# Layer 1 of a two-layer model: rows of four states by 32 channels over segments of 784 columns, on one core

## The chip, the core and the metric

The kernel runs on one core of a Trainium2 chip. The metric is the device time of one execution in microseconds (us). The core has five engines that run their own instruction streams and meet at semaphores: TensorE (PE, with its weight loads as PEld), VectorE (DVE), ScalarE (ACT), GpSimd (POOL) and SyncE (SP), which here issues all DMA transfers. The transfers run on 16 DMA engines. SBUF and PSUM are the memories beside the engines, 128 partitions wide; PSUM is what TensorE writes.

## What is computed

The input x has 16 images of 192 channels and 56 x 56 = 3136 positions. Layer 0 adds a gated recurrence over the positions to x. Layer 1 adds a bidirectional selective scan; the change concerns it alone. Its core, for each of the 384 inner channels d and 16 states n:

```
xc  = silu(conv_b + sum_k xp[:, k:k+L] * conv_w[:, k])       # 4 taps along the positions
dbl = xc @ W_xproj.T                                          # 12 columns for dt, 16 for B, 16 for C
dt  = softplus(dbl[..., :12] @ W_dt.T + dt_bias)
h_t = h_(t-1) * exp(dt_t * A) + (dt_t * x_t) * B_t            # per channel and state
y_t = sum_n h_t * C_t        ;  y = y + xc * D
out = ((y_f + y_b) * silu(z)) @ W_out.T + b_out               # y_f forward, y_b backward over the positions
```

Everything is float32.

## The kernel before

Layer 0 (lines 63 to 535) runs first and leaves two tensors in DRAM: `xmid`, the residual stream, and `xhat`, the normalised input of layer 1.

Layer 1 (from line 541) walks over 224 **steps**: 16 images, forward then backward, 7 segments of T = 448 positions. Each step has 24 **units**: 3 blocks m of 128 channels by 8 pairs p of states. The 128 partitions of a tile are 128 channels, and a unit holds two states side by side, 2 x 448 = 896 columns. For a unit:

- `decay` (L833): ScalarE writes exp(dt * A) for each of the two states into a PSUM tile dA (2 buffers), two instructions.
- `times_b` (L840): GpSimd multiplies the rows of B, broadcast over partitions, with dt*x (tile dtx): dB, 4 buffers.
- `scan` (L845): VectorE runs the recurrence h = dA*h + dB, one instruction a state. The result goes back into dA, or into SBUF tile h for each third unit (`on_pool`).
- `times_c` (L875): h * C gives hC (4 buffers), on VectorE for two units of three and on GpSimd for the third.
- `add_up` (L881): TensorE adds the two states into y of the block by products with the identity, 448 columns each; the block's first unit also adds D * xc and, backward, the forward result yf.
- `keep` (L863): ScalarE copies the last column as the next segment's start.

The order is written by hand (L898 to L916): at iteration u the program issues keep(u-1), decay(u+1), scan(u), times_c, times_b(u+3), add_up(u-2), and then what is listed in `events` for that slot. `prelude(i)` (L645) fills those events. It works one step ahead: slot s of step i falls in the iterations of step i-1. There the input projection px (L668), the convolution pc as four products with diagonal matrices (L688), the gates (three ScalarE instructions in one slot, L637), the projection pp (L725), the write of B and C to DRAM (`bc`, L737) and dt and dtx (L744 to L756) are made, and B and C are read back broadcast over all 128 partitions, two states at a time, with 10 buffers each (`load_rows`, L758). dt and dtx stay in SBUF. After a block's last unit `y_out` (L770) takes y from PSUM; after a backward step `po_mm` and `po_out` make the output.

All engines take their instructions in order, SP too: a load that waits for a buffer holds back every later transfer of that queue. [...]

Of the kernel before, what the change touches and what calls it, by code (L numbers as in the profile page):

```python
# [19 lines left out]
NPR = NS // 2  # L20
DTR = 12
KC = 4
T = 448
# [7 lines left out]
def _bc(ap, n):  # L31

    p, t = ap.shape
    return ap.unsqueeze(1).to_broadcast([p, n, t])
# [3 lines left out]
def tile_wkv_then_bimamba(ctx: ExitStack, tc: tile.TileContext, a: dict, out: bass.AP):  # L38
# [501 lines left out]

    cw = ctx.enter_context(tc.tile_pool(name="l1const", bufs=1))
    ring = ctx.enter_context(tc.tile_pool(name="l1ring", bufs=2))
    pa = ctx.enter_context(tc.tile_pool(name="l1a", bufs=2, space=PSUM))
    py = ctx.enter_context(tc.tile_pool(name="l1y", bufs=2, space=PSUM))
    pm = ctx.enter_context(tc.tile_pool(name="l1mm", bufs=2, space=PSUM))

    ident = cw.tile([128, 128], F32, tag="ident", name="ident")
    make_identity(nc, ident)

# [11 lines left out]
    with tc.tile_pool(name="l1raw", bufs=1) as raw:  # L561
        for n, g, sh in (("W_in_x", "g1", "b1"), ("W_in_z", "g2", "b2")):
            wt = raw.tile([P0, NB0, DI], F32, tag=n, name=n)
            nc.sync.dma_start(out=wt, in_=blocks(a[n]))
            g_t, sh_t = vec(g, [P0, NB0]), vec(sh, [P0, NB0])
            bt = cw.tile([128, NM], F32, tag="bias_" + n, name="bias_" + n)
            for m in range(NM):
                pb = pm.tile([128, 512], F32, tag="mm", name="pb1")
                for c in range(NB0):
                    nc.tensor.matmul(  # L570
                        pb[:, 0:1],
                        wt[:, c, m * 128 : (m + 1) * 128],
                        sh_t[:, c : c + 1],
                        start=c == 0,
                        stop=c == NB0 - 1,
                    )
                nc.vector.tensor_copy(bt[:, m : m + 1], pb[:, 0:1])
            ws = cw.tile([P0, NB0, DI], F32, tag=n + "_g", name=n + "_g")
            for c in range(NB0):
                nc.vector.tensor_scalar(ws[:, c, :], wt[:, c, :], g_t[:, c : c + 1], None, ALU.mult)  # L580
            Win[n], bin_[n] = ws, bt
# [7 lines left out]
    for d in "fb":  # L589
        w = {}  # L590
        cwt = vec(f"conv_w_{d}", [128, NM, KC])
        w["diag"] = cw.tile([128, NM, KC, 128], F32, tag="diag" + d, name="diag" + d)
        for m in range(NM):
            for j in range(KC):
                nc.vector.tensor_scalar(w["diag"][:, m, j, :], ident, cwt[:, m, j : j + 1], None, ALU.mult)
# [9 lines left out]
        w["dtw"] = cw.tile([DTR + 1, DI], F32, tag="dtw" + d, name="dtw" + d)  # L605
        nc.sync.dma_start(out=w["dtw"][0:DTR, :], in_=a[f"W_dt_{d}"])
        for m in range(NM):
            nc.sync.dma_start(
                out=w["dtw"][DTR : DTR + 1, m * 128 : (m + 1) * 128],
                in_=a[f"dt_bias_{d}"][:, m : m + 1].rearrange("p m -> m p"),  # L610
            )
        al = vec(f"A_log_{d}", [128, NM, NS])
        w["A"] = cw.tile([128, NM, NS], F32, tag="A" + d, name="A" + d)
        nc.scalar.activation(w["A"], al, AF.Exp)
        nc.vector.tensor_scalar(w["A"], w["A"], -1.0, None, ALU.mult)
        br.append(w)
    dtr2 = []
    for i in range(2):
        t = cw.tile([DTR + 1, T], F32, tag=f"dtr{i}", name=f"dtr{i}")
        nc.gpsimd.memset(t, 1.0)  # L620
        dtr2.append(t)

    TH = T + KC - 1
    NU = NM * NPR
# [9 lines left out]
    def mm_tile(name):  # L634
        return pm.tile([128, 512], F32, tag="mm", name=name)

    def silu_gate(name, ps, nbias):  # L637

        g = ring.tile([128, T], F32, tag="gate", name=name)
        nc.scalar.activation(g, ps, AF.Exp, bias=nbias, scale=-1.0)  # L640
        nc.scalar.activation(g, g, AF.Ln, bias=1.0)
        nc.scalar.activation(g, g, AF.Exp, scale=-1.0)
        return g

    def prelude(i):  # L645
# [6 lines left out]

        lo, hi = (t0, min(L, t0 + TH)) if bwd else (max(0, t0 - (KC - 1)), t0 + T)
        n = hi - lo
        off = TH - n if not bwd else 0
        st["own"] = 0 if bwd else n - T
        st["xs"], st["xc"], st["dt"], st["dtx"], st["z"] = {}, {}, {}, {}, {}
        st["Bt"], st["Ct"], st["yf"], st["ys"] = {}, {}, {}, {}
# [5 lines left out]
        def load_xh():  # L664
            st["xh"] = ring.tile([P0, NB0, TH], F32, tag="xh", name="xh")
            nc.sync.dma_start(out=st["xh"][:, :, :n], in_=blocks(xhat_d[b])[:, :, lo:hi])

        def px_mm(m):  # L668
            tmp["px", m] = px = mm_tile("px")
            for c in range(NB0):  # L670
                nc.tensor.matmul(  # L671
                    px[:, :n],
                    Win["W_in_x"][:, c, m * 128 : (m + 1) * 128],
                    st["xh"][:, c, :n],
                    start=c == 0,
                    stop=c == NB0 - 1,
                )

        def px_out(m):
            st["xs"][m] = xs = ring.tile([128, TH], F32, tag="xs", name="xs")  # L680
            if n < TH:
                pad = slice(n, TH) if bwd else slice(0, off)
                nc.gpsimd.memset(xs[:, pad], 0.0)
            nc.scalar.activation(
                xs[:, off : off + n], tmp["px", m][:, :n], AF.Identity, bias=bin_["W_in_x"][:, m : m + 1]
            )

        def pc_mm(m):  # L688
            tmp["pc", m] = pc = mm_tile("pc")
            for j in range(KC):  # L690
                o = KC - 1 - j if bwd else j
                nc.tensor.matmul(  # L692
                    pc[:, :T], w["diag"][:, m, j, :], st["xs"][m][:, o : o + T], start=j == 0, stop=j == KC - 1
                )

        def pc_gate(m):
            tmp["gc", m] = silu_gate("gc", tmp["pc", m][:, :T], w["ncb"][:, m : m + 1])

        def pc_out(m):
            st["xc"][m] = xc = ring.tile([128, T], F32, tag="xc", name="xc", bufs=4)  # L700
            nc.vector.scalar_tensor_tensor(
                xc, tmp["pc", m][:, :T], w["cb"][:, m : m + 1], tmp["gc", m], ALU.add, ALU.mult
            )

        def pz_mm(m):
            tmp["pz", m] = pz = mm_tile("pz")
            for c in range(NB0):
                nc.tensor.matmul(
                    pz[:, :T],
                    Win["W_in_z"][:, c, m * 128 : (m + 1) * 128],  # L710
                    st["xh"][:, c, st["own"] : st["own"] + T],
                    start=c == 0,
                    stop=c == NB0 - 1,
                )

        def pz_gate(m):
            tmp["gz", m] = silu_gate("gz", tmp["pz", m][:, :T], nbz[:, m : m + 1])

        def pz_out(m):
            st["z"][m] = z = ring.tile([128, T], F32, tag="z", name="z")  # L720
            nc.vector.scalar_tensor_tensor(
                z, tmp["pz", m][:, :T], bz[:, m : m + 1], tmp["gz", m], ALU.add, ALU.mult
            )

        def pp_mm():  # L725
            tmp["pp"] = pp = mm_tile("pp")
            for m in range(NM):
                nc.tensor.matmul(
                    pp[: 2 * NS + DTR, :T], w["xp"][:, m, :], st["xc"][m], start=m == 0, stop=m == NM - 1
                )  # L730

        def pp_out():
            bcs = ring.tile([2 * NS, T], F32, tag="bcs", name="bcs", bufs=1)
            nc.scalar.copy(bcs, tmp["pp"][0 : 2 * NS, :T])
            nc.scalar.copy(dtr2[i % 2][0:DTR, :], tmp["pp"][2 * NS : 2 * NS + DTR, :T])
            st["bc"] = dramr.tile([2 * NS, T], F32, tag="bc", name="bc")
            nc.sync.dma_start(out=st["bc"], in_=bcs)  # L737

        def pd_mm(m):
            tmp["pd", m] = pd = mm_tile("pd")  # L740
            nc.tensor.matmul(pd[:, :T], w["dtw"][:, m * 128 : (m + 1) * 128], dtr2[i % 2], start=True, stop=True)


        def pd_log(m):  # L744
            tmp["ab", m] = ab = ring.tile([128, T], F32, tag="ab", name="ab")
            nc.scalar.activation(ab, tmp["pd", m][:, :T], AF.Abs)
# [3 lines left out]
        def pd_out(m):  # L750
            st["dt"][m] = dt = ring.tile([128, T], F32, tag="dt", name="dt", bufs=4)
            nc.vector.scalar_tensor_tensor(dt, tmp["pd", m][:, :T], 0.0, tmp["ab", m], ALU.max, ALU.add)  # L752

        def dtx(m):
            st["dtx"][m] = t = ring.tile([128, T], F32, tag="dtx", name="dtx", bufs=4)
            nc.gpsimd.tensor_tensor(t, st["dt"][m], st["xc"][m], ALU.mult)  # L756

        def load_rows(which, p, first):  # L758
            st[which][p] = t = ring.tile([128, 2, T], F32, tag=which, name=which, bufs=10)
            nc.sync.dma_start(out=t, in_=st["bc"][first + 2 * p : first + 2 * p + 2, :].partition_broadcast(128))  # L760

        def load_yf(m):
            st["yf"][m] = t = ring.tile([128, T], F32, tag="yf", name="yf_t")
# [6 lines left out]
        def y_out(m):  # L770
            st["ys"][m] = ys = ring.tile([128, T], F32, tag="ys", name="ys", bufs=4)
            if bwd:
                nc.vector.tensor_tensor(ys, st["y", m][:, :T], st["z"][m], ALU.mult)
                return
            nc.scalar.copy(ys, st["y", m][:, :T])
# [4 lines left out]
        def po_mm(k):  # L780
            tmp["po", k] = po = mm_tile("po")
            for m in range(NM):
                nc.tensor.matmul(
                    po[:P0, :T], Wout[:, m, k * P0 : (k + 1) * P0], st["ys"][m], start=m == 0, stop=m == NM - 1
                )

        def po_out(k):
            if k == 0:
                st["o"] = ring.tile([P0, NB0, T], F32, tag="o", name="o", bufs=1)
            nc.vector.scalar_tensor_tensor(  # L790
                st["o"][:, k, :], tmp["po", k][:P0, :T], bout[:, k : k + 1], st["xmid"][:, k, :], ALU.add, ALU.add
# [177 lines left out]
```

## Time and profile before

| | |
|---|---|
| median of 3 runs | 22,529.4 us (22,524.35 to 22,530.25) |
| profiled execution, its own time | 22,528.8 us |
| its span, first to last instruction | 22,527.0 us |
| mean granted TensorE clock | 0.892 |
| busy: PE, PEld, DVE, ACT, POOL | 82%, 39%, 87%, 57%, 78% |
| DMA: moved, mean | 2557.58 MB, 114 GB/s |
| loads of B and of C (L760) | 2 x 1792 of 448 KB, 6.8 and 6.6 us to landing |

The span is that of one profiled execution. A group of the profile's part 5 gives line, engine, operation, output and inputs with shapes, count, then busy time in us and the mean of one in ns, then the engine's idle time before such instructions and what ended it. In the list of waits the columns are total us, how often, and the longest. In the table by stage each engine has its busy us and its number of instructions; DMA share is the mean busy share of the 16 DMA engines.

### The profile page before, as it was taken

Reading aid. Unit: us, or ns where it says so; the run is one execution under the profiler, and the core shown is the slowest. Engines: PE = TensorE matmul, PEld = TensorE weight load, DVE = VectorE, ACT = ScalarE, POOL = GpSimd, SP = SyncE. Lnnn points to the kernel's source line nnn. Section 1 sums busy time; section 2 is a strip of 40 time slices with the busy share of each in tenths; the row PEclk is TensorE's granted clock in tenths of the full one; section 3 lists DMA queues with packets and bytes.
Section 4 is the critical chain, followed back from the end, with each engine's and each line's share of the span. In section 5 each row is a group of like instructions: output and inputs, shape, how many; then the busy total and the mean of one; then the engine's idle time right before and its main releaser. Section 6 shows DMA issues by size and latency. Waiting matters only on the chain.

```text
span 22527.0 us, 170276 instructions
## 1 busy us (share of the span) xinstructions
PE 18553.1 (82%) x44630; PEld 8710.7 (39%) x44630; DVE 19655.0 (87%) x19088; ACT 12947.8 (57%) x24169; POOL 17544.7 (78%) x9098
## 2 busy tenths in 40 slices
PE   4666666688888888888888888988888888888888
PEld 2333333334343434343434343434343434343433
DVE  5666666499999999999999999999999999999999
ACT  3444544466665656565656565656565656565655
POOL 3455455388888888888888888888888888888888
PEclk7888887889898989898989898989898989898989
DMA  3444443333333333333323333333332333232332
GB/s 119 142 138 142 139 140 130 103 114 104 115 102 114 105 113 105 112 107 109 110 108 112 107 112 107 112 107 112 107 112 107 112 107 112 107 112 107 112 107 98
DMA packets 982787, 2557.58 MB, mean 114 GB/s; under 512 B 120344, under 2 KB 449328, under 8 KB 981808
## 3 DMA queue, kind: packets, MB, share of 16 engines
q1 hardware_dynamic: 981808, 2546.68, 32.8%
q8 instruction: 351, 5.75, 0.1%
q14 instruction: 628, 5.14, 0.1%
HBM read 2186.57 MB, written 359.66 MB: 113 GB/s over the span
## 4 chain that ended last, share of the span: by engine, by line
PE 39%; DVE 36%; ACT 9%; issue 7%; POOL 5%; DMA 2%; SPq 1%; DVEq 0%; POOLq 0%; ACTq 0%
DVE dA L854 18%; PE y L889 16%; PE pc L692 8%; ACT dA L838 6%; DVE h L854 5%; DVE hC L879 5%; PE px L671 5%; PE pc L109 2%; POOL dB L843 2%; PE pWk L109 2%; POOL hC L879 2%; DVE dt L752 2%; DVE q L336 2%; PE pWv L109 1%; PE y L885 1%
## 5 line engine op out<-in xcount | busy, mean ns | idle before, releaser
L843 POOL TENSOR_TENSOR dB<-Bt,dtx 128x896 f32<-128x896 f32 x5376 | 11169.9, 2083 | 2585.8 <-DVE h L854 1283.9
L889 PE MATMUL y<-hC,ident 128*128 128x448 f32 x21504 | 9762.7, 600 | 2221.4 <-POOL hC L879 2176.8
L854 DVE TENSOR_TENSOR_SCAN dA<-dA,state,dB 128x448 f32<-128x448 f32 x6144 | 7081.2, 1153 | 669.0 <-ACT dA L838 537.2
L889 PEld LDWEIGHTS y<-hC,ident 128*128 128x128 f32 x21504 | 4295.7, 207 | 7168.8 <-issue 3841.5
L879 DVE TENSOR_TENSOR hC<-dA,Ct 128x896 f32<-128x896 f32 x3584 | 3912.6, 1092 | 321.3 <-DVE dA L854 7.2
L838 ACT ACTIVATE dA<-dt,Ab 128x448 f32<-128x448 f32 x5376 | 3422.5, 637 | 1133.3 <-DVE h L854 565.2
L838 ACT ACTIVATE dA<-dt,Af 128x448 f32<-128x448 f32 x5376 | 3421.5, 637 | 805.3 <-DVE hC L879 357.2
L879 POOL TENSOR_TENSOR hC<-h,Ct 128x896 f32<-128x896 f32 x1792 | 3732.9, 2083 | 13.7 <-issue 8.4
L854 DVE TENSOR_TENSOR_SCAN h<-dA,state,dB 128x448 f32<-128x448 f32 x3072 | 3351.0, 1132 | 0.0
L873 ACT COPY state<-dA 128x2 f32<-128x2 f32 x3072 | 485.1, 158 | 4048.5 <-DVE hC L879 4046.5
L336 DVE TENSOR_TENSOR_SCAN q<-a,q,b 128x392 f32<-128x392 f32 x384 | 496.0, 1345 | 903.4 <-ACT b L358 903.4
L671 PE MATMUL px<-xh,W_in_x_g 96*128 96x451 f32 (+1 forms) x2688 | 1239.4, 586 | 26.8 <-DMA xh<-xhat 26.8
L854 DVE TENSOR_TENSOR_SCAN dA<-dA,dB 128x448 f32<-128x448 f32 x1024 | 1119.4, 1093 | 132.5 <-ACT dA L838 105.8
L377 POOL TENSOR_TENSOR gin<-gin,v 128x1176 f32<-128x1176 f32 x128 | 392.0, 3062 | 925.7 <-ACT gin L371 921.7
L692 PE MATMUL pc<-xs,diagf 128*128 128x448 f32 x2688 | 1067.4, 539 | 2.8 <-issue 1.8
L692 PE MATMUL pc<-xs,diagb 128*128 128x448 f32 x2688 | 1065.3, 538 | 0.0
L671 PEld LDWEIGHTS px<-xh,W_in_x_g 96*128 96x128 f32 x2688 | 589.7, 219 | 676.3 <-issue 615.3
L109 PE MATMUL pc<-v,center_w 128*128 128x392 f32 x896 | 433.5, 652 | 446.7 <-DVE v L393 438.5
L756 POOL TENSOR_TENSOR dtx<-dt,xc 128x448 f32<-128x448 f32 x672 | 761.3, 1133 | 19.8 <-DVE dt L752 19.8
L692 PEld LDWEIGHTS pc<-xs,diagf 128*128 128x128 f32 x2688 | 510.3, 190 | 506.6 <-issue 494.0
L692 PEld LDWEIGHTS pc<-xs,diagb 128*128 128x128 f32 x2688 | 508.3, 189 | 504.3 <-issue 479.8
L109 PE MATMUL pc<-xm,center_w 128*128 128x392 f32 x896 | 352.9, 547 | 401.4 <-POOL xm L263 401.1
(156 smaller groups left out, 20434.8 us busy)
## 6 DMA issues: line engine op xcount, KB each, us to landing
Bt<-bc SPq DMA_DIRECT2D x1792, 448.0 KB, 6.8
Ct<-bc SPq DMA_DIRECT2D x1792, 448.0 KB, 6.6
v<-Wv SPq DMA_DIRECT2D x128, 588.0 KB, 5.1
yf<-ys SPq DMA_DIRECT2D x336, 224.0 KB, 1.9
yf_t<-yf SPq DMA_DIRECT2D x336, 224.0 KB, 5.8
xh<-xhat SPq DMA_DIRECT2D x192, 338.2 KB, 6.6
Wk<-k SPq DMA_DIRECT2D x64, 588.0 KB, 3.0
Wv<-ve SPq DMA_DIRECT2D x64, 588.0 KB, 2.9
```

What stands on the lines that cost most here:

```text
L109: nc.tensor.matmul(dst[:, o, :n], wt[:, i, o, :], src[:, i, :n], start=i == ins[0], stop=i == ins[-1])
L336: nc.vector.tensor_tensor_scan(t[:, b, after][:, run], data0(b), data1(b), t[:, b, col : col + 1], op0, op1)
L671: nc.tensor.matmul(px[:, :n], Win["W_in_x"][:, c, m * 128 : (m + 1) * 128], st["xh"][:, c, :n], start=c == 0, stop=c == NB0 - 1,)
L692: nc.tensor.matmul(pc[:, :T], w["diag"][:, m, j, :], st["xs"][m][:, o : o + T], start=j == 0, stop=j == KC - 1)
L752: nc.vector.scalar_tensor_tensor(dt, tmp["pd", m][:, :T], 0.0, tmp["ab", m], ALU.max, ALU.add)
L756: nc.gpsimd.tensor_tensor(t, st["dt"][m], st["xc"][m], ALU.mult)
L838: nc.scalar.activation(dA[u][:, j, :T], st["dt"][m], AF.Exp, scale=br[st["bwd"]]["A"][:, m, n : n + 1])
L843: nc.gpsimd.tensor_tensor(dB[u], st["Bt"][p], _bc(st["dtx"][m], 2), ALU.mult)
L854: nc.vector.tensor_tensor_scan(hs[u][:, j, run], dA[u][:, j, :T][:, run], dB[u][:, j, run], 0.0 if st["first"] else st["before"][:, n : n ...
L873: nc.scalar.copy(nxt["before"][:, n : n + 2].unsqueeze(2), hs[u][:, :, end : end + 1])
L879: eng.tensor_tensor(hC[u], hs[u], st["Ct"][p], ALU.mult)
L889: nc.tensor.matmul(st["y", m][:, :T], ident, hC[u][:, j, :], start=False, stop=p == NPR - 1 and j == 1)
```

## The change

The rows of a tile are no longer 128 channels but four states by 32 channels: partition 32*j + c holds state 4k + j of channel 32q + c of block m. A unit is (m, k, q), k and q from 0 to 3, so 48 units a step, and a segment has T = 784 positions in place of 448, so 4 segments and 128 steps. A unit has one decay, one scan and one product each of 784 columns.

What follows from the layout:

- dt and dtx are needed four times over, once for each state row. They are made as before (128 channels, GpSimd and VectorE), written to DRAM (`dt_d`, `dtx_d`), and read back by `load_rep`, 32 channels repeated fourfold, 4 loads a block each, rings of 6.
- B and C are read back by `load_rows`, four states each repeated for 32 channels, 4 loads each a step, rings of 5.
- The sum over states is a product with `fold`, a 128 x 32 matrix that adds the four state rows of a channel. It writes 32 of the 128 output partitions (column group q of TensorE). Two units are added in one call, with their products alternating between two column groups, in two halves of 392 columns.
- The convolution does the same: xs is written to DRAM with three zero columns at each end, and `load_xs` reads 32 channels shifted by 0 to 3 columns into the four groups of 32 rows (ring of 4); one product with the taps on `fold` replaces four. The input projection is made in forward steps only, since the backward pass reads the same xs.
- One PSUM tile of two banks serves all products of the prelude, and one y. Each gate is split over two slots. times_b runs two units ahead, not three; hC has 5 buffers. B, C and dt columns share one tile.
- The weights are laid out anew at the start of layer 1 with some 130 small loads more.

The diff, cut to its core:

```diff
-T = 448
+T = 784
-def _bc(ap, n):
+def _bc(ap, n, at=1):
     p, t = ap.shape
-    return ap.unsqueeze(1).to_broadcast([p, n, t])
+    return ap.unsqueeze(at).to_broadcast([p, n, t] if at else [n, p, t])
...
-    py = ctx.enter_context(tc.tile_pool(name="l1y", bufs=2, space=PSUM))
-    pm = ctx.enter_context(tc.tile_pool(name="l1mm", bufs=2, space=PSUM))
+    py = ctx.enter_context(tc.tile_pool(name="l1y", bufs=1, space=PSUM))
+    pm = ctx.enter_context(tc.tile_pool(name="l1mm", bufs=1, space=PSUM))
+    HB = T // 2
+    NQ = 4
+    fold = cw.tile([128, 32], F32, tag="fold", name="fold")
...
         def px_out(m):
+            t = row("xin", 1)
...
+            nc.sync.dma_start(out=xs_b[m * 128 : (m + 1) * 128, PAD + t0 : PAD + t0 + T], in_=t)
+        def load_xs(m, q):
+            st["xs"][m, q] = t = row("xs", 4)
+            c0 = m * 128 + q * 32
+            o = t0 + (PAD if bwd else 0)
+            one = xs_b[c0 : c0 + 32, o : o + T]
+            nc.sync.dma_start(out=t, in_=bass.AP(one.tensor, one.offset, [[1, KC], *one.ap]))
         def pc_mm(m):
...
+            for h in range(2):
+                for q in range(NQ):
+                    nc.tensor.matmul(
+                        pc[32 * q : 32 * q + 32, h, :HB],
+                        w["conv"][:, m, q, :],
+                        st["xs"][m, q][:, h * HB : (h + 1) * HB],
...
+                        tile_position=(0, 32 * q),
+                    )
...
         def pd_out(m):
...
+            nc.sync.dma_start(out=st["dt_d"][m * 128 : (m + 1) * 128, :], in_=dt)
         def dtx(m):
...
+            nc.sync.dma_start(out=st["dtx_d"][m * 128 : (m + 1) * 128, :], in_=t)
+        def load_rep(which, m, q):
+            st[which][m, q] = t = row(which, 6)
+            c0 = m * 128 + q * 32
+            nc.sync.dma_start(out=t, in_=_bc(st[which + "_d"][c0 : c0 + 32, :], NQ, 0))
+        def load_rows(which, k, first):
+            st[which][k] = t = row(which, 5)
+            n = first + NQ * k
+            nc.sync.dma_start(out=t, in_=_bc(st["bc"][n : n + NQ, :], 32))
...
+        for m, slot in enumerate((11, 19, 23)):
+            for q in range(NQ):
+                at(slot - (5 if m == 0 else 3), load_xs, m, q)
+            at(slot, pc_mm, m)
...
+        for m, slot in enumerate((29, 37, 41)):
+            at(slot, pd_mm, m)
+            at(slot + 1, pd_abs, m)
+            at(slot + 2, pd_log, m)
+            at(slot + 3, pd_out, m)
+            at(slot + 4, dtx, m)
+        for k in range(NQ):
+            at(32 if k == 0 else 36 + 4 * k, load_rows, "Bt", k, 0)
+            at(33 if k == 0 else 36 + 4 * k, load_rows, "Ct", k, NS)
         for m in range(NM):
+            for q in range(NQ):
+                at(NU + 16 * m + (q - 8 if q < 2 else q - 6), load_rep, "dt", m, q)
+                at(NU + 16 * m + (q - 8 if q < 2 else q - 6), load_rep, "dtx", m, q)
+            at(NU + 16 * m + 19, y_out, m)
+    units = [(st, m, k, q) for st in steps for m in range(NM) for k in range(NQ) for q in range(NQ)]
...
     def decay(u):
+        st, m, k, q = units[u]
+        dA[u] = pa.tile([128, 1024], F32, tag="dA", name="dA")
+        nc.scalar.activation(dA[u][:, :T], st["dt"][m, q], AF.Exp, scale=br[st["bwd"]]["A"][:, m, q, k : k + 1])
     def times_b(u):
+        st, m, k, q = units[u]
+        dB[u] = row("dB", 4)
+        nc.gpsimd.tensor_tensor(dB[u], st["Bt"][k], st["dtx"][m, q], ALU.mult)
...
+    def add_up(us):
+        for h in range(2):
+            cols = slice(h * HB, (h + 1) * HB)
+            for u in us:
+                st, m, k, q = units[u]
+                if k == 0 and q == 0 and h == 0:
+                    st["y", m] = py.tile([128, 2, 512], F32, tag="y", name="y")
+                terms = [(fold, hC[u])]
...
+                for j, (wt, rhs) in enumerate(terms):
+                    nc.tensor.matmul(
+                        st["y", m][32 * q : 32 * q + 32, h, :HB],
+                        wt,
+                        rhs[:, cols],
...
+                        tile_position=(0, 32 * q),
+                    )
...
-            if 0 <= u + 3 < N:
-                times_b(u + 3)
+            if 0 <= u + 2 < N:
+                times_b(u + 2)
...
-            if 0 <= u - 2 < N:
-                add_up(u - 2)
             for fn in events.pop(u, ()):
                 fn()
+            if 0 <= u - 2 < N and u % 2 == 1:
+                add_up((u - 3, u - 2))
```

## Prediction

> **What bounds the kernel now.** I read the totals first, then layer 1 by stage, then who waits for whom, then the costliest groups, and last the DMA queue in a short stretch.
>
> Page, part 1, and busy time by stage (layer 1 begins near 4400 us):
>
> ```profile
> PE 18553.1 (82%) x44630; PEld 8710.7 (39%) x44630; DVE 19655.0 (87%) x19088; ACT 12947.8 (57%) x24169; POOL 17544.7 (78%) x9098
> 4400.00:13000.00 8600.00, 7480.91 (x17464) 3386.08 (x17465) 7987.68 (x7854) 5159.19 (x10372) 7349.34 (x3769) 0.91 0.31 109
> 13000.00:22480.00 9480.00, 8294.31 (x19424) 3756.53 (x19423) 8848.84 (x8703) 5702.70 (x11461) 8108.91 (x4155) 0.92 0.31 109
> ```
>
> Columns of the last two: stretch, length, PE, PEld, DVE, ACT, POOL busy, clock, DMA share, GB/s. Layer 1 takes 22,527 - 4400 = 18,127 us. VectorE is busy 93% of it, GpSimd 86%, the DMA engines 31%. Layer 0 (4400 us) is not touched.
>
> VectorE's waits from 13000 to 22480 us:
>
> ```profile
> DVE dA L854 <- ACT dA L838: 341.9, 371, 1.2
> DVE xc L701 <- ACT gc L642: 44.1, 75, 1.2
> ...
> DVE dA L854 <- POOL dB L843: 3.5, 3, 1.2
> ```
>
> It waits for a decay now and then, for GpSimd hardly ever, and for no transfer. VectorE bounds layer 1.
>
> Groups:
>
> ```profile
> L843 POOL TENSOR_TENSOR dB<-Bt,dtx 128x896 f32<-128x896 f32 x5376 | 11169.9, 2083 | 2585.8 <-DVE h L854 1283.9
> L889 PE MATMUL y<-hC,ident 128*128 128x448 f32 x21504 | 9762.7, 600 | 2221.4 <-POOL hC L879 2176.8
> L854 DVE TENSOR_TENSOR_SCAN dA<-dA,state,dB 128x448 f32<-128x448 f32 x6144 | 7081.2, 1153 | 669.0 <-ACT dA L838 537.2
> L879 DVE TENSOR_TENSOR hC<-dA,Ct 128x896 f32<-128x896 f32 x3584 | 3912.6, 1092 | 321.3 <-DVE dA L854 7.2
> L854 DVE TENSOR_TENSOR_SCAN h<-dA,state,dB 128x448 f32<-128x448 f32 x3072 | 3351.0, 1132 | 0.0
> ```
>
> DMA queue over the whole span, then in 40 slices of 5 us from 13000 to 13200 us:
>
> ```profile
> q1 hardware_dynamic: 981808, 2546.68, 32.8%
> DMA  0000000599885400000000036998680000000000
> GB/s 0 2 3 0 0 0 14 170 288 407 295 344 193 116 3 0 0 0 0 0 2 0 0 83 149 324 402 315 259 277 22 0 0 0 0 0 0 3 2 0
> ```
>
> Transfers come in bursts that fill all 16 engines. One engine moves 2546.68 MB / (0.328 x 16 x 22,527 us) = 21.5 GB/s in the mean, and 407/16 = 25.4 GB/s in the best slice.
>
> **The change, part by part.** Steps fall from 224 to 128, units rise from 5376 to 6144, a unit shrinks from 896 to 784 columns: the columns in all stay the same.
>
> *VectorE.* Rows by length: a product takes 1092 ns at 896 and 607 at 448 (ys, L773), so 1.08 ns a column: 971 at 784. A scan takes 1132 at 448 and 1009 at 392 (s, L336), so 2.2 ns a column: dA 1153 + 336 x 2.2 = 1892, h 1871. Three units now cost 4 x 1153 + 2 x 1132 + 2 x 1092 = 9060 ns, and 2 x 1892 + 1871 + 2 x 971 = 7597 after. Per unit, times units: 16,236 against 15,559 us, a gain of 677. The outputs around them (L701, L721, L752, L773, L790: 1434 us) fall to about 1284: 150. VectorE gains 827 us.
>
> *GpSimd.* 2083 at 896 and 1133 at 448 (L756) give 1846 at 784: 8192 products and 384 of dtx cost 15,832 us against 15,664. That is 168 more, still under VectorE.
>
> *ScalarE.* 10,752 decays of 637 ns become 6144; 336 more columns at the 0.83 ns that 577 (448 columns) and 1177 (1176 columns) give add 280 and make it 917 ns for 784: 6849 falls to 5634. The gates are split over two slots; nothing new comes late here.
>
> *TensorE.* A float32 product shows as two matmuls (21,504 for 10,752). Column-group products: 6144 x 2 halves for the states, 4608 for D and yf, 3072 for the convolution, 19,968 in all; full-width ones 3840. Streaming costs 375 ns per matmul in the trains of the timeline (12 in 4.67 us), so 328 for 392 columns. One after another that is 23,808 x 656 = 15.6 ms; if neighbours in different groups run together, the state part halves. For the overlap the Trainium skill has a rule against it: "TensorE: Matmul & The Clock Gate", Part 3, lets a weight load overlap a running matmul only if their row groups differ, and here all use all rows. The row speaks otherwise: loads of 190 ns on all rows lie inside trains that keep 375 ns. By the row TensorE takes 9 to 16 ms, by the rule 19,968 x 2 x (328 + 130, the pp load of 44 columns) + 2.5 ms = 20.8 ms. I take the row.
>
> *DMA, where I think the time is decided.* The 16 loads of B and C a step (1.6 GB in all) go. In come, per step, 24 fourfold reads of dt and dtx, 8 of B and C, 12 of shifted xs: 44 loads of 128 x 784 x 4 B = 0.401 MB, 17.66 MB. Beside them about 5.5 MB (writes of dt, dtx, xs; xh, yf, xmid, out). That is 23.2 MB x 128 = 2.96 GB. Over 16 engines at 24 GB/s it takes 60 us a step, hidden under VectorE's 125 us (16,870 busy now in layer 1, less 827, over 128 steps). But all 44 loads have a source whose slowest dimension counts 4: load_rep and load_xs repeat or shift 32 rows four times, load_rows takes four rows. Today's loads name 128 or 96 rows first. The Trainium skill, "DMA: Bandwidth & Descriptors" (sections "Why a DMA increments its semaphore by 16 and not by 1" and "Rules for kernel authors"), says a transfer from this queue runs on the largest number of engines up to 16 that divides the slowest dimension of both sides, always the lowest-numbered, and that a leading broadcast of c copies is confined to c engines. No large transfer of this trace has such a shape. A small one is near: the 12-row load of W_dt_f (L606) has one early step in the trace's semaphore records, 0.65 us after issue, and then twelve single landings between 1.5 and 1.9 us; loads of 128 rows show sixteen. So twelve engines carried it.
>
> The two ends: on 16 engines nothing is exposed. On 4, a load takes 0.401/4 = 0.100 MB per engine, 4.0 us at 25.4 GB/s, 4.7 at 21.5. Per step 44 x 4.0 = 174 us to 44 x 4.7 = 205 us, plus 5.5/16 = 0.34 MB of the rest, 14 us. I take 4.2 us (24 GB/s, since fewer engines crowd each other less than in the mean): 184 + 14 = 198 us, 1.6 times VectorE's 125. The DMA engines are then the bound.
>
> The idle of those four: they stand still where SP cannot issue. The xs ring has 4 buffers, so block 2's loads (slot 20) wait for block 1's convolution (slot 19), itself waiting for its loads: some 5 us from its landing to the next issue. Between slots 33 and 40 there is no load but Ct: about 12 us of work missing, of which the writes of dt and dtx fill about 9. That is 8 us a step: 206 us.
>
> Who waits: pc_mm on TensorE for xs; behind it add_up, so the hC ring of 5 stays full and VectorE's products stop; GpSimd's times_b and ScalarE's decay wait for dtx and dt, whose ring of 6 lets only two of the next block's four in early; behind SP's wait for the convolution stand the next block's loads.
>
> *Setup.* About 136 more small loads (A_log by state, taps, zeros) at the 0.5 us that SP takes for each: 75 us, before layer 1's first step, hidden by nothing.
>
> Sum against the profiled execution: 4400 + 75 + 128 x 206 = 30,843 us; its own time (22,528.8) lies 0.6 us from the median of the runs, so nothing is added: **30,850 us**. VectorE's 827 us are hidden.
>
> **Rivals.**
> *The loads use all 16 engines (0.14).* For it: the destination names 128 rows, and a program may cut the source as it likes before it is issued. Against it: the 12-row load, the stated rule. VectorE stays the bound: 18,127 - 827, and of its 18,127 - 16,870 = 1257 us idle about 128/224 remain (540 less), + 75: 16,835 + 4400 = 21,235 us, faster by 6%. The point: 17,660/(24 k) + 14 = 125 us at k = 6.6; from 8 engines on VectorE decides, so this ends on the other side.
> *Column groups don't overlap and their weight loads show (0.04, with 16 engines).* TensorE 20.8 ms: 4400 + 20,800 + 75 = 25,275 us. The change then doesn't do what it says. If the loads are confined as well, 20.8 ms lies under 26.4 and hardly shows.
> *Four engines, with worse or better streaming (within the 0.82).* 174 + 14 without idle: 128 x 188 + 4475 = 28,540; 205 + 14 + 20 idle: 35,070.
>
> **How the numbers follow.** Four engines 0.82, 16 engines 0.14, TensorE bound 0.04. Range 27,500 to 35,000 us: the likeliest case from slightly under its no-idle sum (engines a little above the best slice seen) to its upper end; it leaves out about 0.2. Faster by over 0.2% 0.14, within 0.2% (about what a measurement of this kernel can tell from no change) 0.01, slower 0.85.
>
> **What would show it.** The mean DMA share over 16 engines should be near 28% in layer 1 while loads of 392 KB take well over 8 us to land, with the GB/s of the full slices near 100, not 400; PE waits for DMA xs, POOL for DMA dtx and ACT for DMA dt. VectorE near 60% busy, scans near 1.88 us, GpSimd products near 1.85 us. I am wrong if full slices show 300 GB/s or more: then the loads spread over all engines and VectorE's 93% return, at about 21,235 us. If PE's trains show more than 656 ns per column-group product, its rival holds.

## The result and the profile after

The changed kernel takes 32,341.5 us, the median of four runs (32,321.7 to 32,361.8), against 22,529.8 us before: a ratio of 1.435 (95% interval 1.433 to 1.438). It is slower by 9.8 ms. The forecast was 30,850 us in a range of 27,500 to 35,000. The profiled execution has a span of 32,324.5 us.

First the totals (the page, part 1), then layer 1 by stage, with the same columns as before: stretch, length, busy us of PE, PEld, DVE, ACT and POOL, granted clock, DMA share, GB/s.

```profile
PE 15393.4 (48%) x55286; PEld 5449.0 (17%) x55286; DVE 18855.8 (58%) x14031; ACT 10967.5 (34%) x16457; POOL 17634.8 (55%) x9739
4400.00:16000.00 11600.00, 5184.96 (x19458) 1587.48 (x19460) 6581.54 (x4748) 3660.70 (x5821) 6388.36 (x3519) 0.67 0.29 106
16000.00:32200.00 16200.00, 7397.87 (x27920) 2285.90 (x27916) 9399.54 (x6746) 5201.90 (x8289) 9105.74 (x5015) 0.68 0.30 107
```

VectorE has 799 us less to do than before (18,855.8 against 19,655.0), and is busy 58% of the time where it was 93% of layer 1. No compute engine is a bound any more. The mean DMA share is no help at first sight: 0.29 and 0.30, where it was 0.31.

Who waits for whom, from 16,000 to 32,200 us (total us, how often, the longest):

```profile
POOL dB L903 <- DMA dtx<-dtx_d: 4266.3, 650, 16.7
ACT dA L898 <- DMA dt<-dt_d: 3461.4, 536, 16.8
...
PE pc L730 <- DMA xs<-xs: 2508.6, 643, 16.9
DVE dA L910 <- POOL dB L903: 2490.0, 508, 10.6
...
PE W_in_x L672 <- DMA xh<-xhat: 1756.1, 36, 51.5
DVE h L910 <- POOL dB L903: 1680.3, 224, 15.7
```

Before the change VectorE waited for no transfer. Now it waits for GpSimd, which is not slow but waits itself for dtx; ScalarE waits for dt, TensorE for xs. Each of these chains ends at a transfer.

The groups that answer to those of before:

```profile
L903 POOL TENSOR_TENSOR dB<-Bt,dtx 128x784 f32<-128x784 f32 x6144 | 11248.6, 1854 | 7604.1 <-DMA dtx<-dtx_d 7302.9
L951 PE MATMUL y<-hC,fold 128*32 128x392 f32 x24576 | 6203.1, 623 | 4670.8 <-POOL hC L934 4465.6
L910 DVE TENSOR_TENSOR_SCAN dA<-dA,state,dB 128x784 f32<-128x784 f32 x3072 | 5680.0, 1849 | 4660.4 <-POOL dB L903 3187.7
L934 DVE TENSOR_TENSOR hC<-dA,Ct 128x784 f32<-128x784 f32 x4096 | 3993.7, 975 | 1983.8 <-PE y L951 1605.6
L898 ACT ACTIVATE dA<-dt,Ab 128x784 f32<-128x784 f32 x3072 | 2811.7, 916 | 4161.4 <-DMA dt<-dt_d 2865.5
L910 DVE TENSOR_TENSOR_SCAN h<-dA,state,dB 128x784 f32<-128x784 f32 x1536 | 2830.7, 1843 | 2105.3 <-POOL dB L903 2100.5
```

The durations (first number behind the bar: busy us, then ns each) are those of the forecast within 3%. What has grown is behind the second bar: the idle time before each instruction. GpSimd loses 7.6 ms before its product, nearly all to dtx.

Then the DMA queue over the span, and 40 slices of 6 us from 20,000 to 20,240 us, a little over one step:

```profile
q1 hardware_dynamic: 1279920, 3548.07, 30.6%
DMA  2252103224252222221222333232350223322326
GB/s 107 100 162 104 59 23 122 86 103 165 95 197 102 101 101 102 102 102 44 74 102 103 119 126 112 102 150 102 105 146 18 86 91 145 151 102 102 153 100 160
```

Before, bursts reached 407 GB/s and the queue then stood empty. Now it often stays on a plateau of 102 GB/s at 2 tenths of 16 engines: about four engines' worth, 25.5 GB/s each. From 16,000 to 32,000 us, sampled each 50 ns in the trace, exactly 4 packets (a large one is 3136 bytes, a row of a tile) were in flight 68% of the time, more than 4 in 20%, 1 to 3 in 4%, and none in 8%. A mean share of 30% thus goes together with four packets or more in flight 88% of the time.

The semaphore records of the trace show the four one by one: a transfer counts up a semaphore as its parts land. Each load of dt, dtx, xs, B and C now ends with one early step and then four single landings; before, a load of B or C ended with sixteen. The last landing of a dtx load comes 19.2 us after its issue (median). A transfer with sixteen landings is held up as well: of a write of dtx, the twelfth comes after 5.7 us and the last after 16.2 us (medians; 3.9 and 4.6 us in the interleaved kernel below). This fits a write of which four parts stand behind the loads on the same four engines.

A step takes (32,324.5 - 4657.4)/128 = 216 us, from the first sum over states to the end of the span.

### The profile page after: what moved, and what is told of

Same layout as the page of the kernel before. It is cut to its first block, busy times and chain, and to the rows that moved or that the text cites. A ratio compares the mean times of both kernels' runs of the same rounds, so it can differ in the third digit from the quotient of the medians.

```text
span 32324.5 us, 184784 instructions
## 1 busy us (share of the span) xinstructions
PE 15393.4 (48%) x55286; PEld 5449.0 (17%) x55286; DVE 18855.8 (58%) x14031; ACT 10967.5 (34%) x16457; POOL 17634.8 (55%) x9739
## 5 line engine op out<-in xcount | busy, mean ns | idle before, releaser
L903 POOL TENSOR_TENSOR dB<-Bt,dtx 128x784 f32<-128x784 f32 x6144 | 11248.6, 1854 | 7604.1 <-DMA dtx<-dtx_d 7302.9
L951 PE MATMUL y<-hC,fold 128*32 128x392 f32 x24576 | 6203.1, 623 | 4670.8 <-POOL hC L934 4465.6
L910 DVE TENSOR_TENSOR_SCAN dA<-dA,state,dB 128x784 f32<-128x784 f32 x3072 | 5680.0, 1849 | 4660.4 <-POOL dB L903 3187.7
L934 POOL TENSOR_TENSOR hC<-h,Ct 128x784 f32<-128x784 f32 x2048 | 3795.0, 1853 | 3609.5 <-PE y L951 2536.9
L934 DVE TENSOR_TENSOR hC<-dA,Ct 128x784 f32<-128x784 f32 x4096 | 3993.7, 975 | 1983.8 <-PE y L951 1605.6
L898 ACT ACTIVATE dA<-dt,Ab 128x784 f32<-128x784 f32 x3072 | 2811.7, 916 | 4161.4 <-DMA dt<-dt_d 2865.5
L898 ACT ACTIVATE dA<-dt,Af 128x784 f32<-128x784 f32 x3072 | 2811.7, 916 | 4124.2 <-DMA dt<-dt_d 3088.1
L910 DVE TENSOR_TENSOR_SCAN h<-dA,state,dB 128x784 f32<-128x784 f32 x1536 | 2830.7, 1843 | 2105.3 <-POOL dB L903 2100.5
L951 PEld LDWEIGHTS y<-hC,fold 128*32 128x32 f32 x24576 | 1647.4, 130 | 8384.3 <-POOL hC L934 5207.5
L910 DVE TENSOR_TENSOR_SCAN dA<-dA,dB 128x784 f32<-128x784 f32 x1024 | 1832.8, 1790 | 1487.1 <-POOL dB L903 1099.0
```

Of the source, the lines that this page charges most:

```text
L898: nc.scalar.activation(dA[u][:, :T], st["dt"][m, q], AF.Exp, scale=br[st["bwd"]]["A"][:, m, q, k : k + 1])
L903: nc.gpsimd.tensor_tensor(dB[u], st["Bt"][k], st["dtx"][m, q], ALU.mult)
L910: nc.vector.tensor_tensor_scan(hs[u][:, run], dA[u][:, :T][:, run], dB[u][:, run], 0.0 if st["first"] else st["before"][:, n : n + 1], ALU ...
L934: eng.tensor_tensor(hC[u], hs[u], st["Ct"][k], ALU.mult)
L951: nc.tensor.matmul(st["y", m][32 * q : 32 * q + 32, h, :HB], wt, rhs[:, cols], start=k == 0 and j == 0, stop=k == NQ - 1, tile_position=(0 ...
```

## The experiments

The theory: the slowest dimension of a load's source sets how many DMA engines carry it; with 4 there, the 44 loads of a step fill four engines. The rivals: it is the bytes and their way through DRAM and SP's queue, or TensorE's column groups. Nine kernels follow in the order of what they settle; a time without an interval is a single run. The edits are cut to the lines, or to the arguments, that change.

**The same bytes, another order of names.** The tiles' partitions become 4 * channel + state in place of 32 * state + channel. Each load is then the same transfer with 32 ahead in its source:

```diff
-  in_=bass.AP(one.tensor, one.offset, [[1, KC], *one.ap])
+  in_=bass.AP(one.tensor, one.offset, [one.ap[0], [1, KC], one.ap[1]])
-  in_=_bc(st[which + "_d"][c0 : c0 + 32, :], NQ, 0)
+  in_=_bc(st[which + "_d"][c0 : c0 + 32, :], NQ)
-  in_=_bc(st["bc"][n : n + NQ, :], 32)
+  in_=_bc(st["bc"][n : n + NQ, :], 32, 0)
```

`fold`, the taps and A are laid out to match; in the setup that is 80 small loads fewer.

> The changed kernel with the rows of a tile in the other order: partition 4c + j in place of 32j + c (c of 32 channels, j of 4 states or taps). Each load keeps its bytes, its 128 packets of 3136 B, its slot, its waits and its buffers; only the slowest dimension of its source is now 32 and not 4. Theory (the engines that carry a load follow from the slowest dimension of its source, so four in the changed kernel): loads land in 3 to 6 us, full slices show 300 GB/s and more, VectorE is the bound again: 21,000 to 22,000 us, near 21,235. Rival 1 (what costs is the way through DRAM itself: 2.96 GB, waits for landings, SP's order): nothing of it changes, 31,500 to 32,500 us. Rival 2 (TensorE in column groups): nothing of it changes, 32,300 us.

Measured: 21,978.5 us (21,968.0 to 21,992.6), 0.975 of the kernel before (0.974 to 0.977). The stage from 12,000 to 21,000 us, two groups, and the issues of dtx (KB each, us to landing):

```profile
12000.00:21000.00 9000.00, 5861.83 (x24550) 1997.36 (x24552) 8198.67 (x5929) 4597.28 (x7250) 8009.47 (x4412) 0.78 0.50 170
L905 POOL TENSOR_TENSOR dB<-Bt,dtx 128x784 f32<-128x784 f32 x6144 | 11258.2, 1865 | 180.3 <-DVE dA L912 138.8
L953 PE MATMUL y<-hC,fold 128*32 128x392 f32 x24576 | 5966.5, 594 | 2182.1 <-POOL hC L936 1925.5
dtx<-dtx_d SPq DMA_DIRECT2D x1536, 392.0 KB, 6.2
```

VectorE is back at 91%, GpSimd's idle before dB falls from 7604 to 180 us, and the same 392 KB land 6.2 us after issue, in place of 19.2, with sixteen landings a load. Slices reach 380 GB/s again (from 15,000 to 15,200 us). The matrix products and the bytes are those of the change. So bytes and column groups fall as the main cause: with the same of both the step takes 136 us. The time lies at the upper end of the theory's range, 740 us over its point. This version beats both kernels.

**Half the engines.** Each load is cut in two DMAs of 64 rows, whose source begins with 2; bytes and packets stay. For dt and dtx:

```diff
-  in_=_bc(st[which + "_d"][c0 : c0 + 32, :], NQ, 0)
+  for g in range(2):
+      src = _bc(st[which + "_d"][c0 : c0 + 32, :], 2, 0)
+      nc.sync.dma_start(out=t[64 * g : 64 * g + 64, :], in_=src)
```

> The changed kernel with each of the 44 loads of a step made as two DMAs of 64 rows, whose source has 2 as its slowest dimension; all bytes and all packets stay as they are. Theory (the slowest dimension of the source sets the number of DMA engines, and 3136-byte packets take 125 ns each): two engines carry a load, 64 packets each, 8.0 us in place of 4.0. A step takes 44 x 8.0 + 14 + 26 = 392 us in place of 217, the program 4600 + 128 x 392 = 54,800 us (50,000 to 57,000), with plateaus near 52 GB/s and a DMA share near 20%. Rival (the time is set by the order of the transfers in SP's queue, by DRAM reads of the same row, or by the size of the loads): same bytes in smaller pieces give 32,300 us or less, as smaller pieces did where each was 32 rows.

Measured: 53,267 us. The DMA queue from 30,000 us, 40 slices of 6 us:

```profile
DMA  1121011111111111112114102111211211112111
GB/s 51 51 110 47 24 50 52 52 51 51 52 50 53 51 51 50 65 52 110 51 51 160 60 24 88 45 52 52 110 50 60 100 51 51 51 52 110 50 51 51
```

The plateau has halved to 51 GB/s. Most moments (85%) have two packets in flight, and each load ends with two single landings. The step takes (53,265.4 - 4777.3)/128 = 379 us: 44 x 8.0 + 14 = 366, and 13 left over as idle (the 14 for all other transfers is the prediction's estimate). Halving the engines does what the theory forecast. The rival, by which smaller pieces are no worse, does not hold.

**All loads as four DMAs of 32 rows**, the layout unchanged, so that each source begins with 32. For dt and dtx:

```diff
-  in_=_bc(st[which + "_d"][c0 : c0 + 32, :], NQ, 0)
+  for j in range(NQ):
+      nc.sync.dma_start(out=t[32 * j : 32 * j + 32, :], in_=st[which + "_d"][c0 : c0 + 32, :])
```

> The changed kernel in its own layout, with each of the 44 loads of a step (dt, dtx, B and C, xs) issued as four loads of 32 partitions, one for each state or tap. Same bytes, same packets, 176 issues in place of 44. Theory of the engine count: each piece names 32 rows first and goes over 16 engines: 21,000 to 22,500 us, at the upper end if SP, at about 0.4 us an issue or 70 us more a step, comes late. Rival 1 (bytes, landings and SP's order): four times the issues make it no better than 32,300 us, rather worse.

Measured: 22,730 us, 230 us above the theory's range, though 9.6 ms below the change. The layout is not the cause; the way the load is named is. The 98 KB pieces land in 2.5 to 2.9 us. It is 750 us over the interleaved form (3.3%), with four times as many issues in SP's queue. From 12,000 to 21,000 us GpSimd waits 340 us for dtx (13 in the interleaved kernel) and VectorE 306 us for dB (8), which is about the 3.3%. That fits loads that are issued late; no run separates it.

**Only dt and dtx split** (24 of 44 loads), as above.

> The changed kernel with only the 24 fourfold loads of dt and dtx of a step issued as four loads of 32 partitions each; the 20 loads of B, C and xs stay as they are. Theory of the engine count: the first four engines carry 20 x 4.0 us, plus 24 x 1.0 and about 14 of the rest, 118 us a step in place of 190; that is just under VectorE's 125, so with bursts 125 to 150 us a step: 20,600 to 23,700 us, near 22,400. Rival 1: 32,300 us or more.

Measured: 27,883 us, a step of 181 us. The direction is right; the size is missed by 5.5 ms, and the range by 4.2. The 20 loads left on four engines (80 us of a step's work there, 118 with the rest) were expected to hide behind VectorE's 125 us. Waits over the whole span:

```profile
PEld pc L730 <- DMA xs<-xs: 3806.2, 975, 6.5
...
PE pc L730 <- DMA xs<-xs: 3433.1, 1104, 8.7
```

The loads of xs come in bursts and lie in a chain: four xs, the convolution, the next four xs. An xs load still ends with four landings and takes 14.5 us to the last (median; 6.0 in the interleaved kernel). That this chain makes up the whole miss was not tested. Comparing a mean load with a step's length says too little where a burst is in series with the step's preparation.

**The confinement put into the kernel before.** There only the source of the B and C loads is named anew, with 4 ahead; destination and bytes are the same.

```diff
-  in_=st["bc"][first + 2 * p : first + 2 * p + 2, :].partition_broadcast(128)
+  in_=st["bc"][first + 2 * p : first + 2 * p + 2, :].partition_broadcast(32).unsqueeze(0).to_broadcast([4, 32, 2, T])
```

> The kernel before, with one edit: its loads of B and C name their 128-fold broadcast as 4 x 32 in place of 128. Same bytes, same packets, same slots. Theory of the engine count: 16 loads of 448 KB a step on four engines at 4.6 us each, 73 us, plus 3 of the rest, in bursts, against 80.7 us a step now: 80 to 100 us a step, 22,500 to 26,900 us, near 24,000, with full slices near 100 GB/s and landings over 10 us. Rival 1: unchanged at 22,530 us with slices up to 400 GB/s.

Measured: 32,520 us, far beyond the expected range (up to 26,900). The queue from 13,000 us, slices of 5 us, and the largest waits:

```profile
DMA  3521000000002432222222232262200000000233
GB/s 110 167 105 47 5 0 0 0 0 0 0 0 51 120 113 107 105 105 105 104 105 105 105 131 105 105 180 105 82 0 0 0 0 0 0 0 0 70 105 111
ACT xs L684 <- PE px L671: 9505.8, 224, 50.8
PE px L671 <- DMA xh<-xhat: 8645.1, 224, 71.9
```

The plateau of four engines appears in a kernel without any other part of the change: 105 GB/s where the same stretch had up to 407. A load of B ends with four landings in place of sixteen, and takes 20.8 us to the last in place of 6.8. A burst of 16 loads takes 16 x 0.459 MB / 105 GB/s = 70 us. The load of xh for the next step stands behind the burst in SP's queue, and the projections wait for it; burst and preparation run one after the other: 125 us a step, against 81 before. The expectation had let them run side by side.

**Where the idle of the four engines is.** The writes of dt and dtx to DRAM go to GpSimd's queue in place of SP's, both behind the product dtx, so that dt is written later than before.

```diff
-  nc.sync.dma_start(out=st["dt_d"][m * 128 : (m + 1) * 128, :], in_=dt)
-  nc.sync.dma_start(out=st["dtx_d"][m * 128 : (m + 1) * 128, :], in_=t)
+  nc.gpsimd.dma_start(out=st["dt_d"][m * 128 : (m + 1) * 128, :], in_=tmp["dt", m])
+  nc.gpsimd.dma_start(out=st["dtx_d"][m * 128 : (m + 1) * 128, :], in_=t)
```

> The changed kernel with the writes of dt and dtx to DRAM issued by GpSimd behind its product dtx, in place of SP; the 44 loads and all bytes stay, and so do the four engines. In the changed kernel's step of 217 us the loads and the rest fill 190 (44 x 4.0 + 14), so 26 stand idle; SP waits 1606 + 942 us of 16,200, or 34 us a step, at those writes, with the loads of B and C behind them. Theory (SP's wait at the writes is most of the idle): the step falls to 195 to 205 us, the program to 29,600 to 30,900 us. Rival 1 (the idle is the ring of four xs and the chain from xs through the convolution to the next xs): 31,800 us or more. Rival 2 (GpSimd's own issues hold up its products): above 32,300 us.

Measured: 30,954 us, 50 us over the theory's upper end. SP's waits in the changed kernel from 16,000 to 32,200 us:

```profile
SPq L797 <- DVE dtc L794: 1606.0, 150, 15.4
SPq L808 <- ACT dA L898: 1036.9, 249, 8.7
SPq L724 <- PE pc L730: 973.5, 75, 13.7
SPq L802 <- POOL dtxc L801: 942.4, 79, 13.4
```

Without the first and the last of these the step is 205.5 us, 10.7 shorter. Taking the writes out of SP's queue thus gives back 41% of the 26 us of idle; the theory was meant to have more than half. The moments without a packet fall from 8% to 5%. The edit does two things at once: SP no longer waits at the writes, and a write of dtx lands after 6.9 us in place of 16.2 (medians). Which of the two the 10.7 us are was not separated, nor what makes up the rest (the chain through the convolution, buffers, packets beside others).

**Column groups one at a time.** In the interleaved kernel the sums are issued unit by unit, in place of alternating.

```diff
-        for h in range(2):
...
-            for u in us:
+        for u in us:
+            for h in range(2):
...
```

> The interleaved kernel (21,978.5 us) with the two units of one sum over states taken one behind the other in TensorE, both halves of one unit and then both of the next, so that neighbouring products lie in one column group. Theory (products of different column groups run together, and TensorE is under its limit here): the mean from start to start of the products of hC with fold rises from 291 ns to 330 or more, TensorE stays under the 17.4 ms of layer 1, and the time stays near 21,980 us, up to 22,400 if VectorE and GpSimd wait longer for the sums. Rival 1 (the groups never ran together): starts and time unchanged to 0.2%. Rival 2 (the overlap is what keeps TensorE off the critical path): 23,000 us or more.

Measured: 22,462.6 us, 0.998 of the kernel before (0.996 to 0.999): 2.2% over the interleaved kernel. This is a miss for all three: the mean from start to start stays (290 ns, 291 in the interleaved kernel), and yet the time rises. That mean is a poor test, since it counts waits. Gaps under 700 ns alone have a mean of 168 ns in the interleaved kernel and 184 here, and in the same 9000 us TensorE is busy 5862 us for 24,550 records there and 6203 us for 23,864 here: 9% more for each. Eight records of sums that stand together (four products of two records each) span 1018 ns from first start to last in the interleaved kernel and 1025 here (medians). One behind the other they would span 7 x 329 = 2303 ns, by the commonest spacing of full-width products (L674) in the same trace. So two records run at a time in either order of issue; which stands beside which, the records do not say. VectorE's waits from 12,000 to 21,000 us, in this kernel:

```profile
DVE xmid_t L843 <- PE po L674: 272.0, 63, 5.8
DVE hC L936 <- PE y L953: 198.6, 131, 3.6
```

In the interleaved kernel the two were 161.1 and 76.5 us. The rise of 233 us in 9000, or 2.6%, is about the 2.2% lost. Why a product costs TensorE more in this order is open.

**Two small trials on the interleaved kernel**: y taken from PSUM a slot earlier (18 for 19), and dB made three units ahead (`times_b(u + 3)`).

> The interleaved kernel with y taken out of PSUM one slot earlier (18 in place of 19); there is one y, so the next block's sums start after it. Theory (a late y holds hC full: GpSimd waits 831 us of 9000 for it, and VectorE loses a part of that): 21,700 to 21,950 us. Rival (VectorE then meets the backward y before its last sums are done and waits there, 129 us of 9000 now): 22,000 to 22,200 us.

> The interleaved kernel with GpSimd's product dB made three units ahead, as before the change, in place of two. Theory (VectorE waits only for decays, sums and the output, not for dB): 21,930 to 22,030 us. Rival (the shorter lead is part of why VectorE is 91% and not 93% busy in layer 1): 21,600 to 21,850 us.

Measured: 21,950.1 us, 0.975 (0.974 to 0.976), and 21,967.3 us, 0.976 (0.975 to 0.977). Neither can be told from the interleaved kernel: the first lies at the upper end of its theory's range, the second inside its own. With the earlier slot, GpSimd's wait for sums falls from 831 to 639 us of 9000, but VectorE's for the backward y rises from 129 to 211. The lead of two units costs nothing there.

## Why the prediction was right, point by point

- **The cause**: right, and shown from both sides: taken away by renaming (21,978 us), brought into the kernel before (32,520), doubled (53,267). The rule of the Trainium skill's page "DMA: Bandwidth & Descriptors" ("Rules for kernel authors"), that a leading broadcast of c copies is confined to at most c engines, could be supported in the trace before only by one 12-row load; the runs agree with it at 2 and at 4: plateaus of 51 and 102 GB/s, two and four landings a load. Nothing between 4 and 16 engines was tried, so the break-even at 6.6 is not shown.
- **A load on four engines**: 4.2 us predicted from 24 GB/s. The median packet of 3136 B takes 125 ns, so 32 of them on each engine 4.0 us, 25.1 GB/s. Of the ends 4.0 and 4.7, the lower was nearer. 44 loads: 176 us for 184.
- **The idle**: 8 us predicted, 26 left over (216 - 176 - 14, the 14 still an estimate). The moments with fewer than four packets in flight agree with it: 11% of a step, 24 us. This is the mis-sized term. The prediction gave the stretch between slots 33 and 40 a net 3 us, since the writes of dt and dtx would fill it. In fact SP waits at these writes (2548 us of 16,200, or 34 us a step) and holds B and C behind them; with the writes out of its queue 10.7 us go. Chains of burst and wait, as in the two misses above, may do the same elsewhere.
- **The sum**: 216 for 206 us a step, about 1300 us of the 1491 between 30,850 and 32,341. Two errors partly cancel here, by luck: the loads were set 8 us too high and the idle 18 too low. The rest is the start: the prediction counts steps from 4475 us, and the first sum comes at 4657.4. It came at 4457.9 before, so 58 of these 182 us are a first preparation that the prediction left out, and 124 are more than the 75 set for the setup (136 loads at 0.5 us would be 68). Setup and a slower first preparation on four engines were not told apart.
- **VectorE**: scans 1849 and 1843 ns for 1892 and 1871, products 975 for 971; 799 us less busy for 827. It is hidden as forecast. **GpSimd** 1854 ns for 1846, **ScalarE** 916 for 917.
- **TensorE**: 12.6 ms busy from 4400 us on, inside 9 to 16. The statement in the Trainium skill's "TensorE: Matmul & The Clock Gate", Part 3, that a weight load overlaps running products only when their row groups differ, would hold the loads back, since all use all rows. It is not what the trace shows: 55,286 loads stand beside 55,286 products, yet full-width products of 392 columns most often start 329 ns apart, with nothing added for the load. The same Part also lets a load go ahead into a background weight buffer, which the prediction left out. The row of the trace was the right choice, and the interleaved kernel (136 us a step) leaves no room for 20.8 ms in layer 1.
- **The rival of 16 engines**: 21,235 us worked out, 21,978 measured once the confinement is gone. Its mechanism is right; it set VectorE's idle too low. VectorE waits for decays (182 us of 9000), the output product (161) and the backward y (129), and stays at 91%.
- **The marks**: the share near 28% (29 to 30%), slices near 100 GB/s, VectorE near 60% (58%) and the three waits for xs, dtx and dt all came. The landings "well over 8 us" came as well: the page after has no time for these loads, but the semaphore records give 19.2 us for dtx, 17.3 for dt and 18.2 for xs (medians).

## What to carry to other kernels

Before a load is laid out, look at which dimension its source names first: the same bytes with 2, 4 or 32 ahead took 379, 216 and 136 us a step here, and the mean DMA share did not give it away, while a flat GB/s plateau and the number of landings a load did. Compare a burst with the slack at its own place in the chain, not a step's mean load with the step's length. A transfer that must wait for an engine holds back all behind it in the same queue; putting two such writes on the queue of the engine that makes one of them and needs the other anyway was worth 1.4 ms.

## What the hardware showed besides

SP itself is held up. An issue of B or C took about 0.4 us before the change (median). On the full queue of the changed kernel an issue can take as long as a load does: 3.7 us for dtx in the median, though 0.5 for B. SP's instructions, one line from before at 13,039 us, then the changed kernel from 20,000 us (start, us):

```profile
13039.25 0.43 SPq L760 DMA_DIRECT2D Ct<-bc  x1
...
19999.53 3.74 SPq L808 DMA_DIRECT2D dtx<-dtx_d  x1
20003.32 3.75 SPq L814 DMA_DIRECT2D Bt<-bc  x1
20007.11 3.81 SPq L814 DMA_DIRECT2D Ct<-bc  x1
20010.97 3.74 SPq L705 DMA_DIRECT2D xh<-xhat  x1
...
20057.75 0.53 SPq L808 DMA_DIRECT2D dt<-dt_d  x1
20058.34 1.16 SPq L808 DMA_DIRECT2D dtx<-dtx_d  x1
```

The issues follow each other at the pace of four engines, one in 3.8 us, as if each waited for room; after a pause they are short again. A landing 19.2 us after issue, at 4.0 us a load, means about five loads under way at once. So a write or a small load in SP's queue can be late even where nothing that it waits for is.

The granted clock of TensorE was lower where TensorE was busy less: 0.89 at 82% before, 0.69 at 48% after, 0.62 at 30% on two engines, 0.78 at 64% interleaved. It does not explain the slowdown: the median record of a sum takes 493 ns in the change and in the interleaved kernel, and TensorE is idle for half of the change's span. VectorE, ScalarE and GpSimd keep their durations: a scan takes 1849 ns in the change, 1850 on two engines and 1845 interleaved.
